# Layer 0 of a two-layer network: half of the scan's sources made by ScalarE and VectorE, small products on GpSimd, PSUM banks assigned by the planner

## The chip, the cores and the metric

The kernel runs on one core of a Trainium2 chip. A core has five engines that work from their own queues, each in order: TensorE (PE, matmuls; its weight loads are listed apart as PEld), VectorE (DVE), ScalarE (ACT), GpSimd (POOL) and SyncE (SP, which issues the DMAs here). They wait for each other through semaphores. On-chip data lies in SBUF, and the matmuls write to PSUM, which has eight banks of 128 x 512 float32. Everything is float32. The metric is the time of one execution on the device in microseconds (us); less is better.

## The reference

The input x is 2 x 2048 x 256 (batch, time, channel). Two layers are applied, each as `x = x + attn(norm(x)) + ffn(norm(x))`. Only layer 0's first branch and its expert network are touched in what they compute with; layer 1 is the larger part of the time.

```python
def _L0_attn_ref(x, W_z, W_params, conv_w, W_dt, b_dt, A_log, D, W_out):
    z = x @ W_z.T
    params = x @ W_params.T                    # dt_unproj (64), unused (16), C (16)
    dt = softplus(dt_unproj @ W_dt.T + b_dt)
    u = silu(causal_conv4(x, conv_w))
    A = -exp(A_log)                            # 256 channels x 16 states
    A_tilde = exp(dt * A)
    B_tilde = where(abs(A) < 1e-05, dt, (A_tilde - 1.0) / (A + 1e-10))
    h[0] = B_tilde[0] * u[0]
    h[t+1] = A_tilde[t] * h[t] + B_tilde[t] * u[t]
    y = sum_n C[t, n] * h[t, :, n]
    return ((y + u * D) * silu(z)) @ W_out.T

def _L0_ffn_ref(x, controller, f1, f2, bias):  # groups of 16 rows, 64 experts
    perm = one_hot_of_best_row(x @ controller)
    inner = relu(select(x, perm) @ f1 + bias)
    return scatter(inner @ f2, perm)
```

Layer 1 has a two-directional selective scan (512 inner channels, 16 states), a feed-forward network behind it, and a network whose dense weights are made from butterfly factors (made in the kernel while layer 0 runs).

## The kernel before

**Layer 0's scan.** Time is cut into chunks of T = 512 steps, four for each of two batches: eight chunks. A scan (L1182) treats 128 rows, 64 channels x 2 states, over 512 steps. The 256 channels are two halves, e = 0 and 1, of two quarters each, h = 0 and 1. For each half and each of eight pairs of states m there is a pair of scans, so 16 pairs, 32 scans, a chunk and 256 in the layer. The kernel walks all eight m of e = 0 first and then those of e = 1. For each pair:

- `load` (L1154 on): SP loads `cb`, two rows of C broadcast to 64 rows each, and `Gm`, the matrix of the sources;
- `decay` (L1150): ACT writes exp(dt A) into a tile of the ring `a` (five tiles of 2 x 512 a row);
- `source` (L1174): PE multiplies `dw` by `Gm` into a PSUM bank of the ring `ab` (two banks). `dw` holds the step of u (u[t+1] - u[t]) in its upper 64 rows and dt u in its lower 64; `Gm` spreads 64 channels over two states and scales each with the inverse of A, or takes dt u where A is tiny;
- `scan` (L1182): DVE runs (source + state) x decay along time;
- `keep` (L1197): POOL saves the last column for the next chunk, and `product` (L1201): POOL multiplies by `cb`;
- `collect` (L1205): PE adds the two states up into a bank `yacc` (one for each half, from a ring of four).

**Around it.** `prepare` makes a chunk's inputs one chunk ahead: projections (PE), `cv`, the convolution (ACT for the first tap, L949, DVE for three more, L962, all in SBUF), silu (L977), softplus (L998), dt u (DVE, L1020), the step of u (DVE, L1029) and a copy of dt u into the lower rows of `dw` (ACT, L1032). `skip` (L1103) starts the bank `yacc` with u D, and the lack products (PE L1115, DVE L1118, PE L1122) correct for the term that the scan leaves out. `gates` and `finish` multiply by silu(z) and by W_out. `prologue` normalizes rows (DVE, L81) and picks the best rows. `experts` runs eight groups of experts: masks (DVE, L680), turned by PE and copied by ACT (L692, L699), gathered rows (L718, L727), two matmuls with a relu (L762, L772, L796, L808), a store to DRAM (`interd<-stage`), a load in another order (`relay<-interd`), and a matmul that is added to the sum (L843, L850). `butterfly_ops` (POOL L281 to L289, DVE L352) makes the weights for layer 1.

**Layer 1's scan** has the same pattern with other names: rows `bT` scaled by ACT (L1847) or POOL (L1849), transposed by PE into `ab` (L1923), scan (DVE L1936), keep and product (POOL L1949, L1955), sum (PE L1967). Its convolution runs in a PSUM bank (ACT L1625, DVE L1632).

**What sets the order.** Nothing loops on the device. Each piece of work is an operation with an engine, an assumed duration, the operations that it needs, the buffers that it takes (`takes`) and a key, its due time in units of one scan (32 a chunk). `Plan.order` places the operations one by one: of those that are ready it takes, for each engine, the one with the lowest key among those that could start within SLACK of the earliest, and then the engine that can start first. An operation that takes buffers isn't started when its key is more than AHEAD0 = 4 beyond the next scan's. The order found is written out engine by engine, and each engine's queue runs in it. Buffers are rings: the n-th taker of a ring of r waits for the users of the (n-r)-th. PSUM is split into rings of fixed banks: `pp` two (all matmuls that are evacuated at once), `ab` two, `yacc` four.

```python
s = op(PE, 1.0, source, ld, ck.o_dw[e], takes="ab", key=key + h - SOURCE0)
before = op(DVE, 1.25, scan, s, (d0, d1)[h], before,
            pv.o_keep[k] if pv and not ck.first else None, key=key + h)
```

## Time and profile before

| | us |
|---|---|
| median of three runs | 2871.68 (2866.61 to 2884.62) |
| the profiled execution | 2875.17 |
| its span, first to last instruction | 2873.5 |
| layer 0's scans (L1182), first and last start | 51.4 and 919.3 |
| layer 1's scans (L1936), first and last start | 930.7 and 2811.5 |

Busy time of the engines in the whole span: PE 2639.9 us (92%), DVE 2378.0 (83%), POOL 2245.8 (78%), ACT 2153.4 (75%). Matmuls overlap and their ends are modelled, so a busy PE is not PE at its peak. A view by stretch gives, for one stretch of the span, each engine's busy us and number of instructions, the TensorE clock that was granted (1.0 is full speed), the share of time in which the DMA engines were busy, and GB/s. A group of instructions is given as line, engine, operation, output<-inputs, shape and count, then busy us and the mean ns of one, then the idle time just before them and what ended it. A waits line says who waited for whom, us in total, how many times and the longest.

### The profile page before, as it was taken

To read this page: it belongs to the slowest core of one execution; us is meant where nothing else is said; L and a number is where in the kernel's file an instruction comes from. 1 tells how busy PE (TensorE), PEld (TensorE's weight loads), DVE (VectorE), ACT (ScalarE), POOL (GpSimd) and SP (SyncE) were. 2 spreads that over 40 slices of the span, in tenths; PEclk is the share of its full clock that TensorE was granted. 3 is DMA by queue.
4 is the path that set the end of the run, shared out by engine and by line. 5 is a ranking of instruction groups with operands and counts; after the bars stand their busy time and mean duration, and the time that the engine had idled before them with its cause. 6 is when DMAs were issued, how large, how long until landed. Compare 5 with 4: busy or idle time off the path is not lost.

```text
span 2873.5 us, 43499 instructions
## 1 busy us (share of the span) xinstructions
PE 2639.9 (92%) x15268; PEld 1877.2 (65%) x15268; DVE 2378.0 (83%) x2508; ACT 2153.4 (75%) x3302; POOL 2245.8 (78%) x2149
## 2 busy tenths in 40 slices
...
GB/s 222 174 205 193 136 189 205 246 203 152 162 181 122 90 82 53 96 68 56 58 99 49 88 85 69 100 74 71 67 60 74 71 56 82 60 64 58 68 63 48
DMA packets 256203, 308.92 MB, mean 108 GB/s; under 512 B 25264, under 2 KB 190256, under 8 KB 254064
## 3 DMA queue, kind: packets, MB, share of 16 engines
...
## 4 chain that ended last, share of the span: by engine, by line
PE 53%; POOL 16%; DVE 14%; issue 7%; DMA 5%; ACT 4%; SPq 1%; POOLq 0%; DVEq 0%; ACTq 0%
PE ab L1923 10%; POOL a L1955 8%; PE yacc L1967 8%; DVE a L1936 6%; PE ab L1174 5%; PE pp L2151 3%; PE pp L2037 3%; PE pp L1607 3%; POOL a L1201 3%; PE pp L2108 3%; PE yacc L1205 2%; PE pp L1578 2%; PE pp L2219 2%; POOL bT L1849 2%; DMA interd<-stage 2%
## 5 line engine op out<-in xcount | busy, mean ns | idle before, releaser
L1955 POOL TENSOR_TENSOR a<-a,cb 128x1024 f32<-128x1024 f32 x512 | 1218.7, 2380 | 29.6 <-DMA cb<-bcd 0.2
L1936 DVE TENSOR_TENSOR_SCAN a<-a,hc,ab 128x512 f32<-128x512 f32 x768 | 941.6, 1264 | 78.2 <-PE ab L1923 60.2
L1905 ACT ACTIVATE a<-dt,A 128x512 f32<-128x512 f32 x1024 | 679.0, 715 | 44.9 <-PE yacc L1967 28.3
L1923 PE MATMUL ab<-ident,bT 128*128 128x128 f32 x4096 | 622.8, 276 | 59.1 <-DVE a L1936 52.6
L1923 PEld LDWEIGHTS ab<-ident,bT 128*128 128x128 f32 x4096 | 484.0, 141 | 240.0 <-DVE a L1936 149.0
L1967 PE MATMUL yacc<-ident,a 128*128 128x128 f32 x4096 | 563.7, 275 | 18.9 <-POOL a L1955 18.6
L1967 PEld LDWEIGHTS yacc<-ident,a 128*128 128x128 f32 x4096 | 471.7, 141 | 58.0 <-POOL a L1955 30.8
L1847 ACT ACTIVATE bT<-dtuT,BT 128x512 f32<-128x512 f32 x640 | 426.1, 713 | 48.2 <-PE ab L1923 45.4
L1936 DVE TENSOR_TENSOR_SCAN a<-a,ab 128x512 f32<-128x512 f32 x256 | 299.1, 1206 | 48.8 <-PE ab L1923 37.2
L1182 DVE TENSOR_TENSOR_SCAN a<-ab,hn,a 128x512 f32<-128x512 f32 x192 | 241.9, 1274 | 97.9 <-PE ab L1174 96.2
L1197 POOL COPY hn<-a 128x2 f32<-128x2 f32 x128 | 47.2, 369 | 344.4 <-DVE a L1182 323.3
L1201 POOL TENSOR_TENSOR a<-a,cb 128x1024 f32<-128x1024 f32 x128 | 306.1, 2391 | 10.4 <-POOL hn L1197 0.3
L1174 PE MATMUL ab<-dw,Gm 128*128 128x512 f32 x512 | 280.9, 646 | 18.1 <-DVE a L1182 9.5
L1150 ACT ACTIVATE a<-dt,As 128x512 f32<-128x512 f32 x256 | 173.6, 716 | 141.1 <-issue 64.9
L1849 POOL TENSOR_SCALAR bT<-dtuT,BT 128x512 f32<-128x512 f32 x384 | 275.0, 721 | 4.8
L1174 PEld LDWEIGHTS ab<-dw,Gm 128*128 128x128 f32 x512 | 86.6, 197 | 143.6 <-issue 64.9
L1949 POOL COPY hc<-a 128x2 f32<-128x2 f32 x512 | 108.5, 212 | 82.6 <-DVE a L1936 80.1
L1205 PE MATMUL yacc<-a,fold 128*64 128x512 f32 x512 | 141.0, 629 | 5.6 <-POOL a L1201 5.6
L2108 PE MATMUL pp<-xnT,wup 128*128 128x256 f32 x512 | 124.6, 388 | 14.8 <-DMA wup<-wupd 12.2
L2037 PE MATMUL pp<-wout,ygT 128*128 128x256 f32 x512 | 130.6, 380 | 2.0 <-DVE zu L1632 1.9
L1607 PE MATMUL pp<-xnT,winx 128*128 128x512 f32 x256 | 125.8, 597 | 2.8 <-DVE zu L1632 2.7
L1578 PE MATMUL pp<-winz,xnT 128*128 128x512 f32 x256 | 125.0, 595 | 2.7 <-DVE zu L1632 2.7
(200 smaller groups left out, 4146.6 us busy)
## 6 DMA issues: line engine op xcount, KB each, us to landing
cb<-bcd SPq DMA_DIRECT2D x256, 256.0 KB, 3.2
cb<-cd SPq DMA_DIRECT2D x256, 128.0 KB, 3.1
Gm<-Gd SPq DMA_DIRECT2D x128, 128.0 KB, 3.2
...
```

The lines of the kernel that those rows point to most:

```text
L1174: nc.tensor.matmul(R["x", h], R["G"][:, h, :], ck.dw[e][:, h, :], start=True, stop=True)
L1182: nc.vector.tensor_tensor_scan(v, R["x", h], v, 0.0 if ck.first else pv.hn[:, k, h : h + 1], ALU.add, ALU.mult,)
L1201: nc.gpsimd.tensor_mul(v, v, R["cb"].unsqueeze(1).broadcast_to([P, 2, T]))
L1607: nc.tensor.matmul(S["ps"], w["winx"][:, k, e * P : (e + 1) * P], ck.xnT[:, k, :], start=(k == 0), stop=(k == 1),)
L1847: nc.scalar.activation(t, ck.dtuT[:, q, :], AF.Copy, scale=v)
L1849: nc.gpsimd.tensor_scalar(t, ck.dtuT[:, q, :], v, 1.0, ALU.mult, ALU.mult)
L1905: nc.scalar.activation(R["a"][:, h], ck.dt[:, e0 + h], AF.Exp, scale=w["A"][:, e0 + h, n : n + 1],)
L1923: nc.tensor.transpose(R["b", h][:, q * P : (q + 1) * P], ck.bT[n, q][:, e * P : (e + 1) * P], c.ident,)
L1936: nc.vector.tensor_tensor_scan(v[:, step], v[:, step], b[:, step], 0.0 if ck.first else pv.hn[:, e, n : n + 1], ALU.mult, ALU.add,)
L1955: nc.gpsimd.tensor_mul(v, v, ck.cb[n].unsqueeze(1).broadcast_to([P, 2, T]))
L1967: nc.tensor.matmul(ck.y[e][:, tb * P : (tb + 1) * P], v[:, tb * P : (tb + 1) * P], c.ident, start=False, stop=(n == NS - 1), is_transpose= ...
L2037: nc.tensor.matmul(S["ps"][:, n * D : (n + 1) * D], ck.ygT[:, e, q * P : (q + 1) * P], ck.w["wout"][:, e, :], start=(e == 0), stop=(e == 3),)
```

## The change

- **Sources.** The scans of a chunk now go through the halves in turn: for each m first e = 0, then e = 1. For e = 0 the source is the matmul as before. For e = 1, ACT copies the step of u (now in all 128 rows of `dw[1]`) into a bank with a scale for each row (`scaled`), and DVE adds `dv` (dt u, in all 128 rows) times a 0/1 factor in the same bank (`rest`). `cb` and `Gm` are loaded once for both halves, and `Gm` exists only for e = 0.
- **Pool.** `ON_POOL = "RRRRRR"` puts six kinds of work from DVE on POOL: the expert masks, dt u of both halves, the step of u of both halves, and the normalization in layer 0's prologue. The second copy of the step (`step_twice`) is there too.
- **Convolution** of layer 0 works in a PSUM bank instead of SBUF; silu of u is an operation for each half, and silu of the gate is one of its own.
- **Banks.** The eight banks are eight fixed tiles. The planner chooses, for each taker, the bank of its list that comes free first, and limits how many whose release isn't placed yet one kind may hold: in layer 0 `pp` up to three of banks 3 to 7, `yacc` banks 0 to 2; in layer 1 `pp` two of banks 4 to 7, `yacc` banks 0 to 3; `ab` two of banks 4 to 7.
- **Rings and due times.** `dt` four tiles instead of three, `dw` four instead of three (a chunk takes three, `dv` among them), `Gm` two instead of three; the lack products' tile comes from the ring `a`. PROD0 1 instead of 0, preparation from key 4 instead of 8, the second batch's experts from key 122, 21 keys each (127, 20), SLACK .08 instead of .15.
- **Layer 1.** `winz` and `wout` lie in another pool and are loaded once layer 0 is done; the two `dt` tiles lie in two pools. All else there is as before, but for the banks and the order.

```diff
-        self.ps = ctx.enter_context(self.tc.tile_pool(name="ps", bufs=2, space=PSUM))
-        self.sums, self.work = sums, work
+    def banks(self, ctx, calls):
+
+        ps = ctx.enter_context(self.tc.tile_pool(name="ps", bufs=1, space=PSUM))
+        self.bank = [ps.tile([P, 512], F32, tag=f"bank{k}", name=f"bank{k}") for k in range(8)]
+        self.calls = calls
...
     def pp(self):
-        return self.ps.tile([P, 512], F32, tag="pp", name="pp", bufs=self.work)
+        return self.bank[self.calls["pp"].pop(0)]
...
-RING0, CB0, LEAD0, LOAD0, SOURCE0, PROD0, COLLECT0, AHEAD0 = 5, 3, 4, 6, 2, 0, 3, 4
-EARLY0, GATE0, PREP0, FIN0, PRO0, EXP0, EXP1, BFLY0 = -2, (10, 15), (8,30), (4, 12), ((-1, 8), (4, 14)), (12, 27), (127, 20), ((8, 110), (114, 200))
+RING0, CB0, XN0, DT0, DW0, GM0, LEAD0, LOAD0, SOURCE0, PROD0, COLLECT0, AHEAD0 = 5, 3, 3, 4, 4, 2, 4, 6, 2, 1, 3, 4
+EARLY0, GATE0, PREP0, FIN0, PRO0, EXP0, EXP1, BFLY0 = -2, (10, 15), (4,30), (4, 12), ((-1, 8), (4, 14)), (12, 27), (122,21), ((8, 110), (114, 200))
...
-SLACK = 0.15
+ON_POOL = "RRRRRR"
+BANKS = {"pp0":((3,4,5,6,7),3),"yacc0":((0,1,2),3),"pp":((4,5,6,7),2),"ab":((4,5,6,7),2),"yacc":((0,1,2,3),4)}
+
+SLACK = .08
...
+        held = {b: None for s, n in self.banks.values() for b in s}
+
+        def free_bank(b):
+            if held[b] is None:
+                return 0.0
+            at = 0.0
+            for u in held[b][0].users[held[b][1]]:
+                if u.end is None:
+                    return None
+                at = max(at, u.end + LATENCY[u.eng])
+            return at
+
+        def choose(o):
+
+            got, at = [], 0.0
+            for t in o.takes:
+                if t not in self.banks:
+                    continue
+                some, most = self.banks[t]
+                have = [b for b in held if held[b] and held[b][1] == t and free_bank(b) is None]
+                if len(have) + [x for x, b in got].count(t) >= most:
+                    return None
+                best = None
+                for b in some:
+                    f = free_bank(b)
+                    if f is not None and b not in [x for y, x in got] and (best is None or f < best[0]):
+                        best = (f, b)
+                if best is None:
+                    return None
+                got.append((t, best[1]))
+                at = max(at, best[0])
+            return at, got
...
-            W["Gd"] = c.dram.tile([P, 4, 8, P], F32, name="Gd")
+            W["Gd"] = c.dram.tile([P, 2, 8, P], F32, name="Gd")
+
+        def rows():
+            W["c1s"], W["smalls"] = inverse(W["As"], "r")
+            nc.vector.tensor_scalar(W["As"], W["As"], -1.0, None, ALU.mult)
...
-        for h in range(4):
+        for h in range(2):
...
-                c.normalize(v, v, *S["m", h], 2)
+                c.normalize(v, v, *S["m", h], 2, nc.gpsimd if ON_POOL[5] == "R" else None)
...
-                nc.vector.tensor_mul(
+                (nc.gpsimd if ON_POOL[0] == "R" else nc.vector).tensor_mul(
...
+        def silu_z():
+            nc.scalar.activation(pv.zs, pv.zs, AF.Silu)
+
+        if i:
+            pv.o_zs = op(ACT, 1.0, silu_z, *pv.o_z, table="silu")
+        us = []
         for e in range(2):
             def conv(e=e):
-                S["c", e] = ap.tile([P, T], F32, tag="cv", name="cv", bufs=rings["cv"])
+                S["c", e] = c.pp()
                 nc.scalar.activation(
...
-            o = op(ACT, 0.67, conv, ck.o_xnT, M["first"], takes="cv")
-            inline("cv", o)
...
-                o = op(DVE, 1.4, tap, o)
+                o = op(DVE, 0.75, tap, o)
...
+
+            def silu_u(e=e):
+                if e == 0:
+                    ck.uw = ap.tile([P, 4, T + 2], F32, tag="uw", name="uw", bufs=rings["uw"])
+                for h in (2 * e, 2 * e + 1):
+                    r = slice(64 * (h % 2), 64 * (h % 2) + 64)
+                    nc.scalar.activation(ck.uw[0:64, h, 2:], S["c", e][r], AF.Silu)
+
+            o = op(ACT, 1.25, silu_u, o, *us, takes="uw" if e == 0 else (), table="silu")
+            c0.users["pp0"].append(o)
+            us.append(o)
...
-                nc.vector.tensor_mul(
+                (nc.gpsimd if ON_POOL[1 + e] == "R" else nc.vector).tensor_mul(
                     ck.uw[64:P, s, 2:], ck.dt[e][0:64, :, 1:], ck.uw[0:64, s, 2:]
...
-                nc.vector.tensor_sub(dw[0:64], ck.uw[0:64, s, 1 : T + 1], ck.uw[0:64, s, 0:T])
+                (nc.gpsimd if ON_POOL[3 + e] == "R" else nc.vector).tensor_sub(dw[0:64], ck.uw[0:64, s, 1 : T + 1], ck.uw[0:64, s, 0:T])
...
-            d = op(DVE, 2.0, delta_u, so, sl)
+            d = op(*((POOL, 2.4) if ON_POOL[1 + e] == "R" else (DVE, 1.5)), delta_u, so, sl)
...
-            d2 = op(DVE, 2.2, step_u, eg, takes="dw")
+            d2 = op(*((POOL, 2.4) if ON_POOL[3 + e] == "R" else (DVE, 2.1)), step_u, eg, takes="dw")
...
-            d3 = op(ACT, 0.99, shift_u, d, d2)
-            ck.o_dw.append(d3)
+            if e == 0:
+                ck.o_dw.append(op(ACT, 0.99, shift_u, d, d2))
+                ck.o_src = list(ck.o_dw)
+            else:
+
+                def step_twice(s=s):
+                    nc.gpsimd.tensor_sub(
+                        ck.dw[1][64:P], ck.uw[0:64, s, 1 : T + 1], ck.uw[0:64, s, 0:T]
+                    )
+
+                def shift_twice(h, s=s):
+                    if h == 0:
+                        ck.dv = ap.tile([P, 2, T], F32, tag="dw", name="dv", bufs=rings["dw"])
+                    nc.scalar.copy(ck.dv[64 * h : 64 * h + 64], ck.uw[64:P, s, 0:T])
+
+                ck.o_step = [d2, op(POOL, 2.4, step_twice, eg, d2)]
+                d3 = op(ACT, 0.99, lambda f=shift_twice: f(0), d, d2, takes="dw")
+                inline("dw", d3)
+                ck.t_dv = d3
+                ck.o_shift = [d3, op(ACT, 0.99, lambda f=shift_twice: f(1), d3)]
+                ck.o_dw += ck.o_step + ck.o_shift
             ck.o_du = d
...
+        ck.t_uw.users["uw"] += [ck.o_uh] + ck.o_dw
...
-                R["t"] = ap.tile([P, 2, T], F32, tag="lk", name="lk", bufs=rings["lk"])
+                R["t"] = sp.tile([P, 2, T], F32, tag="a", name="lk", bufs=rings["a0"])
...
-            s = op(ACT, 1.15, skip, ck.t_uw, M["scans"], takes="yacc", key=key)
+            s = op(ACT, 1.15, skip, ck.o_uw, M["scans"], takes="yacc0", key=key)
             ck.t_y[e] = s
-            inline("yacc", s)
-            m = op(PE, 1.0, lack_mm, ck.o_par, M["cl"], takes=("pp", "pp", "lk"), key=key + 0.2)
+            inline("yacc0", s)
+            m = op(PE, 1.0, lack_mm, ck.o_par, M["cl"], ck.o_du, *ck.o_dw, takes=("pp0", "pp0", "a0"), key=key + 0.2)
+            inline("a0", m)
...
-        for k in range(16):
-            e, m = divmod(k, 8)
-            key = at + 2 * k
+        for j in range(16):
+            m, e = divmod(j, 2)
+            k = 8 * e + m
...
-            def load(e=e, m=m, R=R):
-                R["cb"] = sp.tile([P, T], F32, tag="cb", name="cb", bufs=rings["cb0"])
-                for j in range(2):
...
-            ld = op(SP, 0.2, load, ck.o_cd, *M["G"], takes=("cb0", "G"), key=key - LOAD0)
-            inline("cb0", ld)
+            if e == 0:
+                C = {}
+
+                def load(m=m, C=C):
+                    C["cb"] = sp.tile([P, T], F32, tag="cb", name="cb", bufs=rings["cb0"])
+                    for j in range(2):
+                        nc.sync.dma_start(
...
+                    C["G"] = sp.tile([P, 2, P], F32, tag="G", name="Gm", bufs=rings["G"])
+                    nc.sync.dma_start(C["G"], W["Gd"][:, :, m, :])
+
+                ld = op(SP, 0.2, load, ck.o_cd, *M["G"], takes=("cb0", "G"), key=key - LOAD0)
+                inline("cb0", ld)
...
-                def source(h=h, e=e, R=R):
+                def source(h=h, R=R, C=C):
                     R["x", h] = c.ab()
                     nc.tensor.matmul(
-                        R["x", h], R["G"][:, h, :], ck.dw[e][:, h, :], start=True, stop=True
-                    )
-
-                def scan(h=h, k=k, R=R):
-                    if k == 0 and h == 0:
+                        R["x", h], C["G"][:, h, :], ck.dw[0][:, h, :], start=True, stop=True
+                    )
+
+                def scaled(h=h, m=m, R=R):
+                    R["x", h] = c.ab()
+                    nc.scalar.activation(
+                        R["x", h], ck.dw[1][:, h, :], AF.Copy, scale=W["c1s"][:, 2 + h, m : m + 1]
+                    )
+
+                def rest(h=h, m=m, R=R):
+                    nc.vector.scalar_tensor_tensor(
+                        R["x", h], ck.dv[:, h, :], W["smalls"][:, 2 + h, m : m + 1], R["x", h],
+                        ALU.mult, ALU.add,
+                    )
+
+                def scan(h=h, j=j, k=k, R=R):
+                    if j == 0 and h == 0:
                         ck.hn = ap.tile([P, 16, 2], F32, tag="hn", name="hn", bufs=3)
...
-                s = op(PE, 1.0, source, ld, ck.o_dw[e], takes="ab", key=key + h - SOURCE0)
+                if e == 0:
+                    s = r = op(PE, 1.0, source, ld, *ck.o_src, takes="ab", key=key + h - SOURCE0)
+                    ld.users["G"].append(s)
+                else:
+                    s = op(ACT, 0.62, scaled, *ck.o_step, M["As"], takes="ab", key=key + h - SOURCE0)
+                    r = op(DVE, 0.75, rest, s, *ck.o_shift, key=key + h - 0.6)
+                    ck.t_dv.users["dw"].append(r)
                 inline("ab", s)
                 ck.t_dw[e].users["dw"].append(s)
-                ld.users["G"].append(s)
-                before = op(DVE, 1.25, scan, s, (d0, d1)[h], before,
+                before = op(DVE, 1.25, scan, r, (d0, d1)[h], before,
...
-            def product(R=R):
+            def product(R=R, C=C):
                 v = R["a"]
-                nc.gpsimd.tensor_mul(v, v, R["cb"].unsqueeze(1).broadcast_to([P, 2, T]))
+                nc.gpsimd.tensor_mul(v, v, C["cb"].unsqueeze(1).broadcast_to([P, 2, T]))
...
-            w["winz"] = dp.tile([P, 2, 512], F32, tag="winz", name="winz")
+            w["winz"] = wp.tile([P, 2, 512], F32, tag="winz", name="winz")
...
-        w["z"] = op(SP, 0.2, rows, sw1, *deps)
+        w["z"] = op(SP, 0.2, rows, sw2, *deps)
...
-        w["o"] = op(SP, 0.2, rows, sw1, *deps)
+        w["o"] = op(SP, 0.2, rows, sw2, *deps)
...
-                        ck.dt = ap.tile([P, 4, T], F32, tag="dt", name="dt", bufs=2)
+                        pool = wp if ck.i % 2 else ap
+                        ck.dt = pool.tile([P, 4, T], F32, tag="dt", name="dt", bufs=1)
...
-        "pp": 2, "ab": 2, "yacc": 4, "xp": 1, "lt": 1, "xq": 2, "selT": 1, "pb": 2, "PT": 4,
-        "f1": 1, "f2": 1, "inner": 1, "stage": 2, "relay": 2, "xacc": 4, "xnT0": 3, "zs": 1,
-        "cv": 2, "uw": 1, "par0": 1, "dt0": 3, "dw": 3, "lk": 1, "a0": RING0, "cb0": CB0, "G": 3,
+        "xp": 1, "lt": 1, "xq": 2, "selT": 1, "pb": 2, "PT": 4,
+        "f1": 1, "f2": 1, "inner": 1, "stage": 2, "relay": 2, "xacc": 4, "xnT0": XN0, "zs": 1,
+        "cv": 2, "uw": 1, "par0": 1, "dt0": DT0, "dw": DW0, "lk": 1, "a0": RING0, "cb0": CB0, "G": GM0,
...
+    banks = BANKS
+    pl = Plan(rings, AHEAD0, banks)
+    c.banks(ctx, pl.calls)
```

## The prediction

> **What bounds the kernel now.** I first read the page's busy line and its 40 slices: TensorE is the busiest engine, and the other three lie lower in the first third (layer 0) than in the rest (layer 1). The boundary is dated by the scans: those of layer 0 (L1182) start last at 919.3 us, those of layer 1 (L1936) first at 930.7 us. So the second view is the busy time by stretch: the start (0 to 52), layer 0, layer 1. Columns: stretch, its length, busy us of each engine with the instruction count, granted TensorE clock, DMA share, GB/s.
>
> ```profile
> 0.00:52.00 52.00, 28.10 (x73) 12.38 (x74) 29.86 (x65) 29.03 (x42) 12.22 (x29) 0.70 0.70 227
> 52.00:925.00 873.00, 791.17 (x3282) 371.76 (x3280) 625.80 (x657) 508.95 (x783) 495.31 (x389) 0.96 0.59 182
> 925.00:2873.50 1948.50, 1820.60 (x11914) 1493.10 (x11914) 1722.34 (x1788) 1615.44 (x2479) 1738.23 (x1732) 0.99 0.23 71
> ```
>
> In layer 0 PE is busy 90.6% of the time, DVE 72%, ACT 58%, POOL 57%: one engine is the bound there. In layer 1 it is 93, 88, 83 and 89%: four engines share the load. Adding the four shares gives 2.77 engines busy at once in layer 0 (2421.2 / 873) and 3.54 in layer 1 (6896.6 / 1948.5). Third, the PE groups of 52 to 925, costliest first (busy us, mean ns | idle just before):
>
> ```profile
> L1174 PE MATMUL ab<-dw,Gm 128*128 128x512 f32 x508 | 277.5, 643 | 17.1 <-DVE a L1182 9.5 <-DMA Gm<-Gd 7.4
> L1205 PE MATMUL yacc<-a,fold 128*64 128x512 f32 x512 | 141.0, 629 | 5.6 <-POOL a L1201 5.6
> ```
>
> The largest is the source matmul that this change halves: 254 sources of two records each, 277.5 / 254 = 1.09 us of PE per source. Fourth, the waits, of layer 0 and then of layer 1:
>
> ```profile
> DVE a L1182 <- PE ab L1174: 128.7, 93, 12.4
> ...
> PEld ab L1174 <- DVE a L1182: 52.8, 62, 4.0
> ...
> PE ab L1174 <- DVE a L1182: 9.5, 12, 3.1
> ```
>
> ```profile
> PEld ab L1923 <- DVE a L1936: 149.0, 283, 2.9
> DVE a L1936 <- PE ab L1923: 96.4, 128, 14.6
> ...
> PE ab L1923 <- DVE a L1936: 52.6, 88, 2.7
> ```
>
> Each line gives the waiting row, what it waited for, us in total, times, the longest. The scan waits for a source and the source for a bank that a scan still holds, in both layers: a ring of two banks between PE and DVE.
>
> **The change, part by part (stretch 52 to 925).**
>
> *Sources off PE.* 127 of the 254 sources go: 127 x 1.09 = -139 us of PE, 791 to 652.
>
> *Sources onto ACT and DVE.* Each of the 128 becomes one ACT copy with a scale into a bank and one DVE multiply-add in that bank. The first has no row of its own: SBUF to bank with a scale takes 0.688 us (L1103, 64 rows), SBUF to SBUF 0.72 (L949), bank to bank 0.757 (L1625). I take 0.70: +90 us of ACT. The second has its like in layer 1, one operand in SBUF, the other and the result in a bank:
>
> ```profile
> L962 DVE SCALAR_TENSOR_TENSOR cv<-xnT,cw,cv x48: 719/750/2917, 27.2 to 771.1; 128x512 f32<-128x512 f32 x48
> ```
>
> ```profile
> L1632 DVE SCALAR_TENSOR_TENSOR pp<-xi,pk,pp x128: 726/755/758, 878.1 to 2617.1; 128x512 f32<-128x512 f32 x128
> ```
>
> (min/median/max ns): 0.75 each, +96 us of DVE.
>
> *Convolution into a bank.* The same two rows price it: with all operands in SBUF the tap has the same median but a maximum of 2917 and, in layer 0, a mean of 1299 (54.5 us for 42); in the bank it never passes 758. 42 x 0.75 = 31.5, so -23 us of DVE.
>
> *Masks, norms, dt u and steps to Pool.* DVE loses the groups L680 33.9, L1029 29.0, L81 21.1 and L1020 20.3: -104 us. They too are stretched: L680's median is 684 ns, its mean 1060. POOL gains 32 masks at 1.28 (median of L281, same shape), 32 norms, 16 products and 24 steps (8 of them the second copy). Products and steps run over 1024 elements a partition, as L1201 does (2360 ns): 40 x 2.37 = 95. A 128x256 norm lies between half of L1849 (0.35, 128x512) and L1538 (0.87): I take 0.45, 14 us (11 to 28). POOL +150.
>
> [...]
>
> *Copies and tables on ACT.* 16 copies into dv for 8 copies into dw, at 1.04 (L1032): +8. In the built order ACT loads its function table 148 times instead of 131, because the silu is split in three: 17 x 1.283 (the ACT_TABLE_LOAD rows) = +22.
>
> *DMA.* cb and Gm are loaded once for both halves of the channels: half of 250 x 128 KB and of 124 x 128 KB, 24 of 159 MB. Loads issue ahead of use (3.2 us to landing), and waits on them are few: 13.3 and 6.1 us before the keep copy (L1197), 7.4 before the source (L1174). I count nothing for their being fewer; 27 us is what all present ones cost together.
>
> *Clock.* Stretches of layer 0 show it following PE's load:
>
> ```profile
> 275.00:385.00 110.00, 102.76 (x438) 50.78 (x438) 80.34 (x89) 74.99 (x126) 48.57 (x39) 0.97 0.56 171
> 385.00:495.00 110.00, 93.73 (x388) 45.15 (x389) 78.36 (x86) 58.17 (x88) 60.53 (x50) 0.91 0.64 188
> ```
>
> At 93% busy it is 0.97, at 85% 0.91. With PE busy a little over 80% I take 0.91 against the present 0.96, 5% on 652: +33 us of PE.
>
> [...]
>
> *Sum for layer 0.* PE 652 + 33 = 685; ACT 509 + 90 + 8 + 22 = 629; DVE 626 + 96 - 23 - 104 = 595; POOL 495 + 150 = 645. Together 2554, nothing far ahead any more. How well four such queues overlap decides. At layer 0's present 2.77 it takes 921 us, at layer 1's 3.54 722 (712 without the clock term). I choose 3.25, nearer to layer 1, since the load is now shaped like layer 1's, but below it, because layer 0's expert chain runs through DRAM (PE waits 29.2 us for relay, ACT 17.2 for stage) and takes more table loads per us: 2554 / 3.25 = 786, **-87 us**.
>
> *Change of chunk.* Two channel halves in turn keep both halves' tiles to the chunk's end. A chunk now uses three tiles of the dw ring of four (two of three before), so dv of the next chunk waits for the last scaled copy of this one; the lack products wait for dv, and since their tile now comes out of the decays' ring, the next chunk's first decay waits for them. After the last scaled copy stand two dv copies (2 x 1.04), two skips (2 x 0.69, L1103), four lack matmuls (23.4 us for 32, L1115: 0.73 each, 2.9) and a decay (0.72): 7.1 us, while DVE has one multiply-add and two scans left (3.3). That leaves the scans 3.8 us apart or more at each of seven changes, 27 us; queues in front of these steps can double it, other work can fill it. Nothing of the sort stands in the trace of before. Of 0 to 55 I take **+25**.
>
> *Start.* The first scan (51.4 us) now stands behind three subtractions and a product on POOL (4 x 2.37 = 9.5) where DVE needed 1.22 each for one of either; and the first four lack products stand before it on DVE (they follow it now). Against that, the next scans (57.5 and 64.0) no longer wait for the lacks in between. Between 0 and +10, I take +4.
>
> *Layer 1: banks by schedule.* The same work in the same seam (52 PE and 31 DVE instructions of layer 1 stand ahead of layer 0's last, in both orders). But sources and the other matmuls now draw from four common banks: the built order gives sources three in turn while nothing else needs one. That attacks the waits shown above: at best PE's own 52.6 us go. With PE at 93% and POOL at 89% something else is soon late (POOL's product, L1955). A bank lent to a source can be missed by an evacuation; the list is also re-sorted with a narrower slack. I bound that by 1%, +20. Of -53 to +20 I take **-25**.
>
> Sum: -87 + 25 + 4 - 25 = -83. The profiled run took 2875.2 (span 2873.5 and 1.7 around it), the median of the three is 3.5 lower: 2871.7 - 83 = **2789 us**.
>
> **Rivals.**
>
> *Deep overlap:* layer 0 reaches layer 1's rate (722 or less) and the banks bring 40 or more: -151 + 10 + 4 - 40 = -177, about 2695 (below 2715). For it: layer 1 runs so, with the same two-bank idea. Against: the DRAM chain.
>
> *The ring sets the pace:* PE is relieved, but scans still wait one after another for a source, now through ACT, then DVE; POOL's wait for scans (323.3 us, L1197) shows how much of layer 0 hangs on them. Rate 2.9 for the same work: 881, +8; with the other terms (+25 + 4 - 25): about 2884 (2843 to 2900). That would be a change that relieves PE and doesn't shorten the layer. Against: DVE's 128.7 us wait is on PE's in-order queue, from which half the sources vanish.
>
> *Slower, ACT blocked by banks:* the scaled copy waits on ACT for a bank. Behind it in the same queue stand the decays of later scans, the expert evacuations (L699, L727, L808) and the table loads; DVE waits for the decays, PE for the evacuated banks. Today's waits of sources for a bank are 62.3 us (52.8 + 9.5) for 254, 0.25 each, longest 4.0; at that price 128 cost ACT 31 us. If ACT is otherwise engaged 90% of the time (629 / 0.9 = 699), layer 0 becomes slower by over 1% from (873 + 29 - 4 - 699) / 128 = 1.55 us per copy (the other terms leave +4); at 2 us it is 955: 2872 + 82 + 4, about 2958.
>
> **Chances.** Forecast (2715 to 2843) 0.60; deep overlap 0.14; ring 0.13; ACT blocked 0.13. For 8 in 10 the range takes part of both neighbours: 2690 to 2870. About 1% is what a measurement here can tell from no change (three runs before spread 0.6%); 2843 to 2900 is within it. Faster 0.74, same 0.13, slower 0.13.
>
> **What will show it.** Layer 0's last scan near 860 us instead of 919; PE in layer 0 near 80% with some 140 us fewer source matmuls; scaled copies at 0.70, multiply-adds and taps at 0.75 with no maxima near 3 us; POOL above 80%; clock near 0.91; a gap of some 4 us in the scans at each change of chunk; in layer 1 fewer PE waits on L1936's successor. I am wrong if ACT's waits for DVE in front of the scaled copies pass 1.55 us each, if DVE's wait for sources stays above 130 us, or if layer 1 moves by more than 50.

## The result, and the profile after

The changed kernel takes 2862.1 us (median; 2856.6 to 2873.0) against 2872.7 of the kernel before, measured together on the same chips: ratio **0.9963**, 95% interval 0.9952 to 0.9974. It is faster by 10.5 us, where the forecast was 83. Line numbers below are those of the changed kernel: L1251 is the source matmul, L1257 the scaled copy, L1262 the multiply-add, L1271 the scan, L1187 the lack matmul, L1190 the lack product, L1299 the collecting matmul, L863 the stage copy of an expert's output and L898 the matmul on the relay tile; in layer 1 L2018 is the source, L2031 the scan.

The busy time by stretch of the changed kernel: start, layer 0, layer 1. The columns are those shown before.

```profile
0.00:56.00 56.00, 30.10 (x80) 12.46 (x80) 24.22 (x64) 26.06 (x37) 34.14 (x48) 0.73 0.72 234
56.00:910.00 854.00, 713.30 (x3018) 349.73 (x3019) 595.48 (x695) 604.63 (x929) 584.93 (x476) 0.90 0.49 153
910.00:2860.00 1950.00, 1819.50 (x11912) 1499.00 (x11910) 1727.57 (x1787) 1623.03 (x2489) 1732.76 (x1730) 0.99 0.23 71
```

Layer 0 became 19 us shorter, the start 4 longer, layer 1 did not move. PE lost 78 us of busy time in layer 0, as the step wanted, but the four engines now add up to 2498.3 us in 854, 2.93 at once, where 3.25 was forecast. With 3.25 the same work would have taken 769 us, 85 less; the forecast gave 25 of them to the changes of chunk, apart from this quotient.

The PE groups of layer 0 after (56 to 910): half the source matmuls are gone, and each of the rest, like the collecting matmul, takes longer (665 ns against 643, 673 against 629) at the granted clock of 0.90 (0.96 before).

```profile
L1299 PE MATMUL bank<-a,fold 128*64 128x512 f32 x512 | 154.4, 673 | 30.1 <-POOL a L1295 30.1
L1251 PE MATMUL bank<-dw,Gm 128*128 128x512 f32 x252 | 143.3, 665 | 12.1 <-DVE a L1271 7.6 <-ACT stage L863 1.8 <-ACT PT L754 1.2
```

The waits of layer 0 after (56 to 910):

```profile
POOL hn L1291 <- DVE a L1271: 193.7, 62, 11.1
DVE lk L1190 <- PE bank L1187: 62.3, 14, 13.5
...
ACT stage L863 <- DMA interd<-stage: 44.5, 11, 11.5
...
DVE a L1271 <- PE bank L1251: 42.4, 32, 7.5
...
PE bank L898 <- DMA relay<-interd: 40.4, 12, 6.7
...
DVE bank L1262 <- ACT bank L1257: 24.5, 16, 4.7
...
ACT bank L1257 <- DVE a L1271: 18.2, 18, 4.3
```

The wait that bounded the kernel before, the scan's for a source, fell from 128.7 us to 42.4, and 24.5 of the multiply-adds for their scaled copies. In its place stand a wait of the lack products for their matmuls (9.4 us before, at L1118), and of the stage copy and the relay matmul for their DMAs (17.2 and 29.2 us before).

The scans show where these are. The table adds up, from the trace, the 32 scans of each of layer 0's eight chunks (from the first start to the last end) and the scan-free gaps between chunks, for both kernels:

| us | before | after |
|---|---|---|
| first scan starts | 51.4 | 56.7 |
| inside the eight chunks | 861.7 | 729.6 |
| in the seven gaps between them | 7.3 | 117.3 |
| layer 0's last scan ends | 920.6 | 903.5 |
| from there to layer 1's last scan | 1892.2 | 1896.5 |

The chunks became 132 us shorter and the changes of chunk 110 us longer. The longest gap is the first, 128.0 to 162.5. The timeline of the changed kernel there, PE, then ACT, then DVE (start, duration, engine and line, in brackets the idle time ahead of it and what ended it):

```profile
148.09 1.12 PE L1187 MATMUL bank<-par,cl 16*128 16x512 f32 x2
159.81 2.07 PE L1187 MATMUL bank<-par,cl 16*128 16x512 f32 x2 [10.59 <-ACT stage L863]
...
146.85 1.41 ACT L1175 ACTIVATE bank<-uw,D 64x512 f32<-64x512 f32 x2 [4.65 <-DVE zs L1311]
158.47 1.28 ACT L863 COPY stage<-bank 128x512 f32<-128x512 f32 x2 [10.21 <-DMA interd<-stage]
159.65 2.56 ACT L1224 ACTIVATE a<-dt,As 128x512 f32<-128x512 f32 x4
...
161.91 0.69 DVE L1190 TENSOR_TENSOR lk<-bank,uw 128x512 f32<-128x512 f32 x1 [11.90 <-PE bank L1187]
162.52 2.45 DVE L1271 TENSOR_TENSOR_SCAN a<-bank,hn,a 128x512 f32<-128x512 f32 x2
```

It reads backwards: the scan waits for the lack product and the decay, the product for the second pair of lack matmuls, these for a bank, the bank for a stage copy on ACT, and the copy 10.2 us for the DMA that stores an earlier expert output out of one of the two stage tiles. The decays (L1224) stand behind the same copy on ACT.

### The profile page after: what moved, and what is told of

It reads as the page before. It is cut to its first block, busy times and chain, and to the rows that moved or that the text cites. A ratio compares the mean times of both kernels' runs of the same rounds, so it can differ in the third digit from the quotient of the medians.

```text
span 2860.1 us, 42532 instructions
## 1 busy us (share of the span) xinstructions
PE 2562.9 (90%) x15008; PEld 1861.2 (65%) x15008; DVE 2347.3 (82%) x2545; ACT 2253.7 (79%) x3455; POOL 2351.8 (82%) x2253
## 4 chain that ended last, share of the span: by engine, by line
PE 45%; POOL 22%; DVE 13%; issue 8%; ACT 6%; DMA 5%; SPq 1%; POOLq 0%; DVEq 0%; ACTq 0%
POOL a L2050 11%; PE bank L2018 8%; PE bank L2062 7%; DVE a L2031 4%; PE bank L2246 3%; POOL a L1295 3%; PE bank L2132 3%; PE bank L2203 3%; POOL bT L1944 3%; PE bank L1701 2%; PE bank L1672 2%; PE bank L1299 2%; PE bank L2314 2%; DVE a L1271 2%; DMA interd<-stage 2%
## 5 line engine op out<-in xcount | busy, mean ns | idle before, releaser
L2031 DVE TENSOR_TENSOR_SCAN a<-a,hc,bank 128x512 f32<-128x512 f32 x768 | 930.6, 1260 | 80.0 <-PE bank L2018 62.6
L2018 PE MATMUL bank<-ident,bT 128*128 128x128 f32 x4096 | 613.8, 276 | 33.5 <-DVE a L2031 25.1
L2018 PEld LDWEIGHTS bank<-ident,bT 128*128 128x128 f32 x4096 | 486.7, 142 | 184.1 <-issue 67.3
L2062 PE MATMUL bank<-ident,a 128*128 128x128 f32 x4096 | 565.5, 275 | 33.1 <-POOL a L2050 32.7
L2062 PEld LDWEIGHTS bank<-ident,a 128*128 128x128 f32 x4096 | 470.4, 141 | 77.9 <-POOL a L2050 51.0
L2031 DVE TENSOR_TENSOR_SCAN a<-a,bank 128x512 f32<-128x512 f32 x256 | 295.6, 1202 | 43.4 <-PE bank L2018 34.9
L1295 POOL TENSOR_TENSOR a<-a,cb 128x1024 f32<-128x1024 f32 x128 | 301.8, 2358 | 10.4 <-POOL hn L1291 0.3
L1944 POOL TENSOR_SCALAR bT<-dtuT,BT 128x512 f32<-128x512 f32 x384 | 274.7, 720 | 14.0 <-ACT dtuT L1895 7.5
L1271 DVE TENSOR_TENSOR_SCAN a<-bank,hn,a 128x512 f32<-128x512 f32 x192 | 242.9, 1276 | 38.3 <-PE bank L1251 25.1
L1224 ACT ACTIVATE a<-dt,As 128x512 f32<-128x512 f32 x256 | 174.4, 715 | 21.4 <-PE bank L1299 18.7
L1291 POOL COPY hn<-a 128x2 f32<-128x2 f32 x128 | 27.1, 212 | 194.5 <-DVE a L1271 193.7
L1299 PE MATMUL bank<-a,fold 128*64 128x512 f32 x512 | 154.4, 673 | 30.1 <-POOL a L1295 30.1
L2044 POOL COPY hc<-a 128x2 f32<-128x2 f32 x512 | 107.8, 211 | 82.0 <-DVE a L2031 79.7
L1251 PE MATMUL bank<-dw,Gm 128*128 128x512 f32 x256 | 145.9, 667 | 12.5 <-DVE a L1271 7.6
L2203 PE MATMUL bank<-xnT,wup 128*128 128x256 f32 x512 | 125.5, 387 | 15.2 <-DMA wup<-wupd 12.5
L2132 PE MATMUL bank<-wout,ygT 128*128 128x256 f32 x512 | 128.4, 382 | 3.3 <-ACT h L2323 2.7
L1701 PE MATMUL bank<-xnT,winx 128*128 128x512 f32 x256 | 127.6, 604 | 1.1 <-ACT xnT L1516 0.7
## 6 DMA issues: line engine op xcount, KB each, us to landing
cb<-cd SPq DMA_DIRECT2D x128, 128.0 KB, 3.0
Gm<-Gd SPq DMA_DIRECT2D x64, 128.0 KB, 3.0
```

The lines of the kernel that those rows point to most:

```text
L1271: nc.vector.tensor_tensor_scan(v, R["x", h], v, 0.0 if ck.first else pv.hn[:, k, h : h + 1], ALU.add, ALU.mult,)
L1295: nc.gpsimd.tensor_mul(v, v, C["cb"].unsqueeze(1).broadcast_to([P, 2, T]))
L1299: nc.tensor.matmul(ck.y[e][64 * h : 64 * h + 64], W["fold"], R["a"][:, h], start=False, stop=(m == 7), skip_group_check=True,)
L1944: nc.gpsimd.tensor_scalar(t, ck.dtuT[:, q, :], v, 1.0, ALU.mult, ALU.mult)
L2018: nc.tensor.transpose(R["b", h][:, q * P : (q + 1) * P], ck.bT[n, q][:, e * P : (e + 1) * P], c.ident,)
L2031: nc.vector.tensor_tensor_scan(v[:, step], v[:, step], b[:, step], 0.0 if ck.first else pv.hn[:, e, n : n + 1], ALU.mult, ALU.add,)
```

## The experiments

Four theories of where the forecast's gain went. **A**: the lack products' tile, now out of the decays' ring and tied to the next chunk's copies of dt u, couples the chunks. **B**: POOL's pieces come late. **C**: the stage copy holds a bank while it waits for its DMA; the tile is what is short. **D**: it is the written order. The planner counts a DMA's landing at 2.4 us (`LATENCY`) after an issue of 0.1 to 0.3; the profile of the changed kernel has median landings of 3.0 to 5.3 us for the kinds of layer 0, and the chain that leads into the first gap has one of 8.7 (the stage store issued at 150.4). Each engine's queue runs in order, so an instruction that is placed too early holds up all behind it, as the stage copy above holds up the decays.

All ratios are to the kernel before, with their 95% intervals. "Layer 0" is from the first scan's start to the last one's end, "gaps" as above, "seam" from there to layer 1's first scan, all read from the traces. These three columns are of one profiled execution each, which can lie off the kernel's median (e1 6 us above it, e13 5, e7 10). The kernel before was timed again with each group of runs, at 2870.5 to 2876.3 us, so medians of different groups (e1 to e4, e5 to e8, e9 to e12, e13 to e16, e17 and e18) compare to some 6 us; the ratios allow for that. Line numbers of the edited kernels are off by one, or by some twenty where the sources are on PE; the names tell which row is which.

| | median us | ratio | layer 0 | gaps | seam |
|---|---|---|---|---|---|
| before | 2872.7 | 1 | 869.2 | 7.3 | 10.2 |
| after | 2862.1 | 0.9963 (0.9952–0.9974) | 846.8 | 117.3 | 12.8 |
| e1 control, dt ring 3 | 2866.1 | 0.9977 (0.9963–0.9991) | 852.2 | 151.1 | 14.3 |
| e2 lack tile | 2836.7 | 0.9871 (0.9854–0.9887) | 821.9 | 9.9 | 13.7 |
| e3 four stage tiles | 2833.7 | 0.9867 (0.9849–0.9885) | 811.5 | 107.8 | 13.5 |
| e4 dt u, steps on DVE | 2849.2 | 0.9915 (0.9895–0.9934) | 829.4 | 75.9 | 13.3 |
| e5 lack tile + stage | 2837.6 | 0.9876 (0.9855–0.9897) | 822.8 | 27.7 | 13.7 |
| e6 landing 5.0 | 2838.4 | 0.9878 (0.9855–0.9900) | 804.8 | 122.9 | 12.4 |
| e7 banks of layer 1 fixed | 2890.0 | 1.0064 (1.0031–1.0098) | 857.3 | 113.4 | 13.5 |
| e8 sources on PE | 2875.3 | 1.0010 (0.9997–1.0023) | 855.3 | 108.0 | 12.6 |
| e9 landing 5.0, layer 0 | 2832.5 | 0.9852 (0.9836–0.9869) | 813.7 | 124.1 | 11.3 |
| e10 before, landing 5.0 | 2868.5 | 0.9985 (0.9974–0.9996) | 848.5 | 12.6 | 27.1 |
| e11 = e8 + landing | 2861.8 | 0.9960 (0.9945–0.9974) | 841.7 | 122.7 | 14.3 |
| e12 = lack tile + landing | 2817.5 | 0.9807 (0.9792–0.9822) | 783.4 | 3.9 | 37.8 |
| e13 = e12, banks fixed | 2851.2 | 0.9927 (0.9907–0.9946) | 818.7 | 4.3 | 12.2 |
| e14 = e12, sources on PE | 2814.9 | 0.9808 (0.9792–0.9823) | 800.2 | 8.8 | 12.0 |
| e15 = e12 + stage | 2815.7 | 0.9808 (0.9789–0.9827) | 803.4 | 40.6 | 17.1 |
| e16 = e12, norms on DVE | 2811.7 | 0.9801 (0.9783–0.9819) | 797.9 | 3.1 | 12.5 |
| e17 = e14, the six kinds on DVE | 2814.0 | 0.9784 (0.9767–0.9800) | 800.7 | 8.3 | 11.8 |
| e18 = e12, the six kinds on DVE | 2811.4 | 0.9774 (0.9755–0.9792) | 803.3 | 6.4 | 12.2 |

### The gaps themselves: e1 to e5

e1, a control, since the lack tile needs the room of one dt tile:

```diff
-RING0, CB0, XN0, DT0, DW0, GM0, LEAD0, LOAD0, SOURCE0, PROD0, COLLECT0, AHEAD0 = 5, 3, 3, 4, 4, 2, 4, 6, 2, 1, 3, 4
+RING0, CB0, XN0, DT0, DW0, GM0, LEAD0, LOAD0, SOURCE0, PROD0, COLLECT0, AHEAD0 = 5, 3, 3, 3, 4, 2, 4, 6, 2, 1, 3, 4
```

> The changed kernel with the ring of dt tiles back at three (four in the change); it makes the room that the next two runs need and is their control. All theories: within 15 us of the changed kernel's 2862, scan gaps at the seven changes of chunk still near 117 us in all.

e2, e1 and the lack products in a tile of their own, their matmuls no longer behind the copies of dt u:

```diff
-                R["t"] = sp.tile([P, 2, T], F32, tag="a", name="lk", bufs=rings["a0"])
+                R["t"] = ap.tile([P, 2, T], F32, tag="lk", name="lk", bufs=rings["lk"])
...
-            m = op(PE, 1.0, lack_mm, ck.o_par, M["cl"], ck.o_du, *ck.o_dw, takes=("pp0", "pp0", "a0"), key=key + 0.2)
-            inline("a0", m)
+            m = op(PE, 1.0, lack_mm, ck.o_par, M["cl"], takes=("pp0", "pp0", "lk"), key=key + 0.2)
```

> dt ring three; the lack products have a tile of their own again, their matmuls wait only for the projection (as before the change), and so the next chunk's first decays no longer wait for dv and the steps of u. Theory A (lack tile in the decays' ring couples the chunks): the gaps fall from 117 to under 40 us, time about 2785 (2770 to 2805). Theory B (POOL is late with the steps and dt u): the first scaled copies still wait for them, gaps stay over 90, time over 2845. Theory C (a bank held by the expert store keeps PE's queue): gaps over 80, time over 2835.

e3, e1 and four stage tiles instead of two:

```diff
-        "f1": 1, "f2": 1, "inner": 1, "stage": 2,
+        "f1": 1, "f2": 1, "inner": 1, "stage": 4,
```

> dt ring three; four tiles for the experts' store instead of two, so that ACT's evacuation waits less for the store to land. Theory C: the gaps fall by a third or more (117 to under 80), ACT's wait for the store from 44 to under 15 us, time about 2825. Theories A and B: gaps within 15 us of 117, time within 15 us of the control.

e4, the changed kernel with dt u and the steps on DVE again:

```diff
-ON_POOL = "RRRRRR"
+ON_POOL = "RVVVVR"
```

> dt u and the first copy of the step of u of both halves back on DVE; the second copy of the step stays on POOL. Theory B: gaps fall under 60 us, time about 2805. Theory A: dv still waits for the last scaled copy and the decays for the lack products, gaps within 25 us of 117; time 2850 to 2880, since DVE's stretched products come back (some 50 us of DVE).

The control is 4 us slower than the changed kernel. e2 takes the gaps away, as A has it (151 to 10), but layer 0 gains only 30 us on the control, and the time is 2836.7 where A expected 2785: the chunks grow from 701 to 812 us. In e1's gaps PE is busy for 107 of the 151 us, some 43 of them with the experts' matmuls; in e2 this work lies inside the chunks. e3 gains 41 in layer 0 and leaves the gaps at 108 (151 in the control), so C is right about the time more than about the gaps. A gap in the scans is not lost time as such; other work fills most of it. In e4 the gaps fall to 76 and the kernel gains 13, with 32 us less of POOL and 40 more of DVE: outside what either A or B expected, and not a sign that DVE was short, nor that POOL alone is the cause.

e5, e2 and a third stage tile (cb ring of two for room):

> Both cures of the runs before together: the lack products in a tile of their own (lack matmuls no longer behind the copies of dt u) and a third stage tile for the expert store; dt ring of three as in the control, cb ring of two to make room. Measured alone against the control of 2866.1 us: the first 2836.7 (-29.4), the second 2833.7 (-32.5). If the tile that couples the chunks (theory A) and the bank held by a stage copy that waits for its DMA (theory C) are two losses, the gains add: about 2866 - 62 = 2804, layer-0 end near 842 us. If both only open the same place (the first lack matmuls of a chunk), it is about 2830, end near 868. I expect between, 2812.

The two don't add up: 2837.6 against 2836.7 and 2833.7, where the sum would have been 2804. That fits the theory that they open the same place; it doesn't prove it, since e5 has three stage tiles where e3 has four, and a smaller ring of cb.

### The order: e6, e9, e10, e12

e6 alters one number, the planner's landing; e9 does it for layer 0 alone; e10 does the same to the kernel before; e12 is e9 and e2 together:

```diff
-LATENCY = (0.25, 0.2, 0.12, 0.15, 2.4)
+LATENCY = (0.25, 0.2, 0.12, 0.15, 5.0)
```

```diff
+        o.lat = self.lat if eng == SP else LATENCY[eng]
...
+    pl.lat = 5.0
     r, x1_stores, ops0 = layer0(
...
+    pl.lat = LATENCY[SP]
```

> The changed kernel with one number of its planner altered: the time that the planner adds for a DMA's landing is 5.0 us instead of 2.4, so that instructions which need a DMA are placed later in their engine's queue; the computation is the same. Theory D: the in-order queues stand still because the written order puts DMA-fed instructions where the planner thinks the data are there, while landings of 4 to 9 us were seen (stage copy 44.5 us in 11 waits, relay matmul 40.4 in 12). Then the stage copy's and relay's waits fall by over half and the time by 20 to 40 us against the changed kernel's 2862: 2822 to 2842. If the place in the order does not matter because the tile itself is what is short (theory C), or the loss lies in the lack tile (A), the time stays within 8 us of 2862.

> The changed kernel, planner's DMA landing 5.0 us for the operations of layer 0 alone, 2.4 for those of layer 1. With 5.0 everywhere layer 0's last scan ended at 864.6 us (903.5 in the changed kernel) but layer 1 took 1902.5 (1883.8). Theory D (the written order of layer 0 is what loses the overlap): layer 0 ends near 865, layer 1 takes 1884 again, time 2823 +- 6. If the seam between the layers gives it back (layer 1's time grew because layer 0 ended early, not because of its own order): near 2838.

> The kernel before with the same edit of its planner (5.0 us for layer 0's DMAs). Two theories of why the changed kernel overlaps less than forecast. D1: the changed order alone suffers from the landings that are taken too short (before, PE's work hid them: stage copy 17.2 us of waits against 44.5): before moves by less than 10 us, 2863 to 2873, and the change is then worth about 45 us. D2: both orders suffer alike: before gains 25 to 40 too (2832 to 2848), and the change is worth as little as measured, 10 to 20 us.

> The two causes together: lack products in a tile of their own (alone 2836.7, control 2866.1) and layer 0's DMA landings planned at 5.0 us. If they are separate losses: 2866 - 29 - 39 = 2798. If both only fill the same standstill at the chunk's change, as the lack tile and the stage tiles together did (2837.6 against 2836.7 and 2833.7): 2820 to 2835. I expect 2810.

D holds in the main. In e9 the same instructions with the same tiles, in another order, take 33 us less in layer 0 and 30 in all (2832.5, between its two expectations). The landings had not become longer than before the change (median of `interd<-stage` in layer 0: 4.3 us before, 3.3 after); what grew were the waits for them. The two waits named fell, as expected, by over half, from 44.5 and 40.4 us (waits of e9, up to 900):

```profile
ACT stage L864 <- DMA interd<-stage: 16.4, 6, 6.4
...
PE bank L899 <- DMA relay<-interd: 10.4, 7, 3.2
```

The gaps remain (124 us): again they are not the measure. With the larger number in layer 1 too, that part was 15 us longer (e6 1914.9 us from layer 0's end to the last scan, e9 1899.5; one pair).

e10 is D1's forecast in its total (-5.0 us), but not cleanly: its layer 0 became 20.7 us shorter and the seam 16.9 longer. What is firm: the edit is worth 5 us to the kernel before and 30 to the changed one, and the difference between the two grows from 10.5 to 36.

In layer 0, e12 adds up in full: 783.4 us, 63 less than the changed kernel and 86 less than before, more than the 62 that were forecast for the layer with its changes of chunk (its last scan starts at 834.6, the forecast said 860). The seam then gives 25 us back, and the total, 2817.5, falls between the two expectations: layer 1's first scan waits until 873.7. The traces show where the seam's time goes. From layer 1's first projection (L1795; L1701 before) to its first scan takes 23 to 51 us in all twenty kernels. Where the seam is 10 to 15 us, that projection starts 19 to 38 us before layer 0's last scan ends; in e15 it starts 6 us before, in e12 just as that scan ends, and in e10 0.8 us after.

How much a change of order alone can do is shown by e7 and e13 below: they alter only the banks of layer 1, and layer 0 became 10.5 and 35.3 us longer. So one pair of runs 30 us apart would prove little. But the longer landing shortened layer 0 in all five pairs (e6 and e9 against after, e10 against before, e11 against e8, e12 against e2: 42, 33, 21, 14 and 38 us), and the lack tile in both of its pairs (e2 against e1, e12 against e9: 30 and 30).

### What the moves between engines are worth: e8, e11, e14, e16 to e18

e8 leaves the changed kernel but for the sources: all by matmul, no dv, no second step.

```diff
-                if e == 0:
-                    s = r = op(PE, 1.0, source, ld, *ck.o_src, takes="ab", key=key + h - SOURCE0)
-                    ld.users["G"].append(s)
-                else:
-                    s = op(ACT, 0.62, scaled, *ck.o_step, M["As"], takes="ab", key=key + h - SOURCE0)
-                    r = op(DVE, 0.75, rest, s, *ck.o_shift, key=key + h - 0.6)
-                    ck.t_dv.users["dw"].append(r)
+                s = r = op(PE, 1.0, source, ld, ck.o_dw[e], takes="ab", key=key + h - SOURCE0)
+                ld.users["G"].append(s)
```

> The changed kernel with the sources of both halves of the states as matmuls again (Gm for all four quarters, a dw ring of three, no dv copies and no second step on POOL); halves of channels in turn, masks, norms, dt u and the first steps on POOL, taps in banks stay. It puts some 127 x 1.09 = 139 us of PE back and takes 89 us from ACT, 94 from DVE and 15 from POOL (8 x 1.89). If PE set layer 0's pace before and the move of the sources is what shortened the chunks (the prediction's step): PE needs about 850 us at a clock of 0.96 and at its 90.6% of before layer 0 takes 925 to 940, time 2920 to 2945. If the sources were not the bound and the chunk changes are the loss (no dv, so no lack matmul behind the copies): under 2850.

> All sources as matmuls (as in the run with 2875.3 us), with layer 0's DMA landings planned at 5.0 us. The step that takes half the sources off PE was worth 13 us at 2.4. If the order hid its worth, it is larger here: this kernel stays above 2855 (PE 790 us busy in layer 0 can hardly fit 830 us) while the changed kernel with the same planner comes to 2823, a difference of 30 or more. If PE was never what held the layer, the two differ by 13 again: about 2836.

> Both losses mended, and all sources as matmuls on PE. Its difference to 2817.5 is what the move of the sources is worth when the order does not hide it. By the prediction (PE is the bound of the layer) layer 0 cannot take less than its 790 us of PE at 91%, 865: last scan near 905 to 915, time 2855 to 2870, so the move is worth 40 to 50. If PE was not the bound it is within 15 of 2817.

e8 fits neither of its readings. e11 comes out as its first one has it (above 2855, 29 us behind e9 where 30 or more was expected), e14 as its second (within 15 of 2817). The move of half the sources, the first step of the change and of the prediction, is worth 13 us in the order as built (e8 against after), 29 with the landing corrected (e11 against e9) and nothing, -2.6 us, when both losses are mended (e14 against e12). In e14 layer 0 itself is 17 us longer than in e12; the seam is 26 shorter. And e8 has no dv at all and yet 108 us of gaps: dv is not what couples the chunks.

e16 undoes one move to POOL in e12, e17 and e18 all six of `ON_POOL`, in e14 and in e12:

```diff
-ON_POOL = "RRRRRR"
+ON_POOL = "RRRRRV"     (e16)
+ON_POOL = "VVVVVV"     (e17, e18)
```

> Both losses mended and layer 0's 32 norms back on VectorE: POOL loses 39 us (32 x 1.23), DVE gains 15 to 21. If POOL's late arrivals still hold the layer (theory B; POOL 589 of 810 us busy), 5 to 15 us faster: 2803 to 2812. If no engine is the bound and only the order counts, within 6 of 2817 in either direction.

> Both losses mended, all sources on PE, and masks, norms, dt u and steps back on VectorE: what is left of the change in layer 0 is the order (halves of channels in turn), the taps and the choice of banks. If the moves to POOL shorten the layer (the prediction's -104 us of DVE): DVE rises from 504 to some 610 of 800 us, scans and POOL's products come later, time 2830 to 2860. If the order alone did it: within 8 of 2815, that is 2807 to 2823.

> Both losses mended, half the sources on ScalarE and VectorE as in the change, but masks, norms, dt u and steps on VectorE. DVE has then 603 + 104 = 707 us (more where the pieces are stretched beside POOL) in some 800, 88%. If DVE becomes the layer's bound: layer 0 near 830 instead of 783, time 2840 to 2860, and the moves to POOL are what lets the sources leave PE. If nothing is bound: within 10 of 2817.

e16's gain of 6 us (2 by the ratios) is within what both expectations allow, though its first scan does come 5 us earlier (47.3). e17 and e18 are as their second readings have it: the six kinds of work cost the kernel nothing where they were, on DVE (e17 is 0.9 us under e14, e18 6.1 under e12; 7 and 9 by the ratios). Here too layer 0 and the seam share it out: e18's layer 0 is 20 us longer than e12's, its seam 26 shorter. At the prediction's prices the move costs POOL 46 us more than it saves DVE (150 against 104). The rows bear out that POOL is slower (1.89 to 1.22 us for the step, medians of e14 and e17); the times show no gain from the move and a loss of 9 us at most. The busy time by stretch over layer 0 of e12, e14, e17 and e18, in this order:

```profile
52.00:836.00 784.00, 676.81 (x2984) 329.20 (x2981) 595.84 (x699) 603.59 (x923) 582.96 (x478) 0.92 0.53 167
```

```profile
53.00:853.00 800.00, 758.55 (x3275) 366.96 (x3274) 504.91 (x571) 536.64 (x805) 572.89 (x471) 0.98 0.56 176
```

```profile
52.00:856.00 804.00, 760.84 (x3280) 367.64 (x3280) 601.45 (x658) 538.47 (x803) 478.16 (x390) 0.98 0.56 173
```

```profile
47.00:847.00 800.00, 689.70 (x3015) 336.82 (x3013) 691.62 (x783) 616.91 (x941) 484.68 (x391) 0.93 0.53 164
```

Four quite different loads (PE 677 to 761, DVE 505 to 692, POOL 478 to 583, sums of 2373 to 2483) take 784 to 804 us. With the sources on PE that engine is 95% busy, as in layer 1, at a clock of 0.98. The PE work that takes 791 us in the kernel before takes 759 at this clock and fits into 800 us, against 873 before: PE was the busiest engine there, but not what made the layer 873 us long. Of the four only e12 is shorter, by 16 to 20 us; e13 shows that the order alone can move more.

The view that says so was there for the kernel before: the chain, cut to most of layer 0 (57 to 845), by line. First the kernel before, then e17, then e18.

```profile
by line: PE ab L1174 14.0%; issue 9.6%; POOL a L1201 8.6%; PE yacc L1205 6.6%; DMA interd<-stage 6.2%; PE pp L843 5.6%; PE pp L718 4.7%; DMA relay<-interd 3.8%; DMA Gm<-Gd 2.3%; DMA cb<-cd 2.2%; PE pp L762 2.1%; DVE a L1182 2.1%; PE pp L922
```

```profile
by line: PE bank L1231 22.4%; PE bank L1274 11.2%; PE bank L899 7.3%; PE bank L774 5.8%; DMA relay<-interd 4.6%; PE bank L852 3.8%; PE bank L818 3.7%; issue 3.6%; POOL a L1270 3.0%; PE bank L1305 2.8%; DMA interd<-stage 2.6%; PE bank L1117 
```

```profile
by line: POOL a L1295 8.7%; issue 8.2%; DVE a L1271 7.5%; PE bank L1251 6.5%; PE bank L1299 6.4%; PE bank L899 4.8%; PE bank L774 3.7%; PE bank L818 2.6%; DMA interd<-stage 2.6%; PE bank L852 2.3%; POOL bft L330 2.2%; ACT selT L783 2.2%; DV
```

In the kernel before the source matmuls (L1174) are 32% of layer 0's length in busy time, but 14.0% of its chain; DMAs stand in it with 14.5% in the lines named. In e17 (sources L1231) PE's lines come to 57%: there it is the bound. In e18, with half the sources gone, none is: POOL's product, DVE's scan and PE follow one another, and the layer is no shorter.

### The banks of layer 1: e7, e13

```diff
-"pp":((4,5,6,7),2),"ab":((4,5,6,7),2)
+"pp":((4,5),2),"ab":((6,7),2)
```

> The changed kernel with layer 1's banks dealt as before, two for the sources and two for the other matmuls, instead of four chosen by the schedule; layer 0 as changed. The prediction gave the choice of banks -25 us (then about 2887 here); layer 1 was 1882.0 us long before and 1883.8 after, so I now expect no difference: layer 1 within 6 us of 1884, time 2856 to 2868.

> The kernel with both losses mended (lack tile of its own, layer 0's landings planned at 5.0 us: 2817.5) with layer 1's banks dealt two and two. If the choice of banks is worth something of itself, this is 25 or more slower again: 2843. If the +28 of the run before came from one place of its order (second chunk of layer 1, 135.7 us instead of 108.6, where a norm waits for a DMA), the chunks from the third on take the same as in all others (1646 to 1651 us together) and the time stays within 10 of 2817.

e7 missed, and e13 came out as the first of its theories has it: the fixed banks cost 28 and 34 us. Yet layer 1 itself shows little of it. From its third chunk on it takes 1645.8 us before, 1646.0 after, 1651.4 in e7, 1640.3 in e12 and 1651.3 in e13. The profiled executions are 38 and 39 us apart. Of e7's 38, 10 are in layer 0 and 27 in layer 1's second chunk, 135.7 us against 108.6 (its first is 9 shorter), the rest in the later chunks and behind the last scan; of e13's 39 on e12, 35 are in layer 0 and 11 in the later chunks, while seam and first two chunks give 9 back. In e7's second chunk (1047 to 1183) a norm waits for a DMA and the transposes for the norm:

```profile
PE bank L1509 <- DVE xn L82: 8.8, 3, 7.2
...
DVE xn L82 <- DMA yfd<-xn: 6.8, 1, 6.8
```

The kernel before has fixed banks and 110.2 us at this place; e12, with banks by schedule, has 139.8 (after a first chunk of 101). So this stall goes with the written order, which changes with every edit, and not with fixed banks as such. Layer 1's first two chunks together take 256 and 257 us in e7 and e13 and 230 to 244 in all others, the kernel before among them: a loss that the fixed banks have in the changed order alone. Whether the banks have a worth beside that was not separated: layer 0, whose banks e7 and e13 leave alone, moved as much as layer 1.

### A third stage tile on top: e15

e12 and a third stage tile:

> Both losses mended and a third stage tile (cb ring of two to make room). If the stage tile is a loss of its own (ACT waits 10.7 us for the expert store and PE 14.4 for the relay in the mended kernel), up to -15: 2802 to 2812. If the planned landing has already taken it, within 5 of 2817.

Within 2 us of e12, with layer 0 20 us longer and a seam 21 shorter. So no loss of the stage tile's own is seen where the landing is planned right; the smaller ring of cb may hide one.

## Why the prediction was wrong

*Sources off PE, clock.* Right in kind, and the sources in size: 252 source records instead of 508, -134 us (forecast -139); the granted clock 0.90 (0.91). But PE came to 713 us (685): its other work grew by 56, where the clock term had 33. The trace's clock record has 174.1 us at half speed in this stretch, 78.5 in that of before. e14 and e12 show it again: 127 sources fewer, and PE falls by 82 us only (758.55 to 676.81), the collecting matmul going from 624 to 659 ns while the clock goes from 0.98 to 0.92.

*Prices.* The rows of single instructions in the changed kernel (min/median/max ns):

```profile
L1257 ACT ACTIVATE bank<-dw,rc x128: 668/691/723, 56.2 to 897.2; 128x512 f32<-128x512 f32 x128
```

```profile
L1262 DVE SCALAR_TENSOR_TENSOR bank<-dv,rsmall,bank x128: 721/731/757, 59.0 to 901.5; 128x512 f32<-128x512 f32 x128
```

```profile
L1017 DVE SCALAR_TENSOR_TENSOR bank<-xnT,cw,bank x48: 723/755/756, 30.2 to 771.3; 128x512 f32<-128x512 f32 x48
```

```profile
L82 POOL TENSOR_SCALAR xp<-xp,mv,rs x32: 1215/1230/1735, 11.4 to 452.3; 128x256 f32<-128x256 f32 x32
```

```profile
L1073 POOL TENSOR_TENSOR uw<-dt,uw x16: 1992/1996/2069, 44.4 to 798.7; 64x1024 f32<-64x1024 f32 x16
```

Copy, multiply-add and taps are as forecast (0.70, 0.75, 0.75, and the taps' maximum fell from 2917 to 756). The norm on POOL was mis-sized: 1.23 us against 0.45, outside its bounds of 0.35 and 0.87 (the row that fits best is the costlier one, L1538); 32 of them are 39 us, not 14. Products over 64 rows take 2.0 and steps 1.89, not the 2.37 of 128 rows. Since other POOL pieces also became shorter (the keep copy's mean fell from 369 to 212 ns, that of the butterfly's 128x512 product, L281 before, from 1460 to 1338), POOL has 585 us, not 645. DVE is 595 (595), ACT 605 (629). The engine sums were good to 2% in all: 2498 against 2554.

*The rate of 3.25.* **This is the step that failed**, and with the changes of chunk it carries layer 0's part of the error. The two profiled executions differ by 13 us, 70 short of 83: 40 are missing in layer 0 (-22 us by the scans, against -87 + 25), 29 in layer 1 with its seam (+4 against -25), 1 at the start. The quotient itself is further off: 2498 / 3.25 = 769, 85 us under the 854 measured, changes of chunk included. "How well four such queues overlap decides" was put, and then a number between two layers was chosen from the shape of the load. The runs show that the rate is not set by the load's shape: with the same sums (within 2%) it is 2.93 in the built order and 3.14 in e12, and with three other loads it is whatever makes some 800 us (2.97 in e14, 2.96 in e17, 3.10 in e18). In its place stand the order that the planner writes with landings counted too short (33 us in layer 0, e9) and the lack tile (30 us against its control, e2; 30 more on top of e9, e12); mended together they take layer 0 past its forecast. The DRAM chain was named as the reason to choose below 3.54; its waits were 29.2 and 17.2 us before and 40.4 and 44.5 after, and that they would grow was not asked.

*Half the sources as what the layer is worth.* That "one engine is the bound there" was read from 90.6% busy and from the scan's 128.7 us of waits. e14 and e17 keep all sources on PE and take 800 us. The kernel before with the longer landing takes 848.5 (e10). The 48 us between e10 and e17 lie in what e17 has in common with the changed kernel: the halves of channels in turn with their loads made once, the taps in banks, the shared banks of layer 0, and the due times. These were not taken apart.

*Change of chunk.* The mechanism was half right, and its size off: gaps of 117 us instead of 27 to 55, through the lack tile in the decays' ring, but not through dv (108 us without it in e8), and with the stage copy's DMA in the middle, which the chain forecast did not have. Their cost, though, is not their length: taking them away brings 30. That the lack products are the coupling is shown by e2 (gaps 151 to 10).

*Start.* Right: the first scan at 56.7 instead of 51.4, +5 where +4 (0 to 10) was forecast.

*Layer 1's banks, -25.* Wrong: 1892.2 us from layer 0's last scan to the last of all before, 1896.5 after. Of the waits that it attacked PE's for a bank did fall, the scan's for a source did not. Over 1185 to 2800, inside layer 1 in both, the kernel before:

```profile
PEld ab L1923 <- DVE a L1936: 127.2, 236, 2.9
DVE a L1936 <- PE ab L1923: 71.1, 108, 4.0
...
PE ab L1923 <- DVE a L1936: 45.8, 76, 2.7
...
1185.00:2800.00 1615.00, 1536.66 (x10130) 1261.69 (x10129) 1472.24 (x1506) 1388.09 (x2125) 1483.45 (x1474) 1.00 0.23 70
```

and the changed kernel:

```profile
DVE a L2031 <- PE bank L2018: 74.9, 91, 1.9
...
PEld bank L2018 <- DVE a L2031: 57.8, 110, 2.8
...
PEld bank L2062 <- POOL a L2050: 39.4, 58, 1.6
...
PE bank L2018 <- DVE a L2031: 21.8, 44, 2.6
...
1185.00:2800.00 1615.00, 1536.88 (x10125) 1268.27 (x10124) 1477.43 (x1506) 1377.75 (x2109) 1475.80 (x1468) 1.00 0.23 70
```

PE's 173 us of waits became 80, the scan's 71 stayed at 75, and PE did the same 1537 us of work in the same 1615. POOL's product is late more often (39.4 us of waits at L2062, 25.4 before at L1967), as the forecast's own caution said; the weight of that caution should have been the whole term.

*Rivals.* "The ring sets the pace" comes nearest in its number (rate 2.9; 2862 lies in its 2843 to 2900), but not in its cause: the scan's waits for sources fell to 42.4 us. "ACT blocked by banks" is refuted: 18.2 us of waits for 128 scaled copies, 0.14 us each against the 1.55 at which it would decide. "Deep overlap" did not come, nor did e12 reach it in layer 0 (783 us against its 722). None of the three signs of being wrong came up (0.14 us of waits a copy, 42.4 us for sources, layer 1 moved by 4): they watched single waits, and the loss was in none of these. POOL, at 68% of layer 0, stayed under the 80% that was to show the forecast.

*What stays open.* Why layer 0 takes some 800 us in e18, where no engine is over 87%, was not settled; its chain only shows that no line has 9% of it. Nor is it settled why the order of e10 and e12 has layer 1's first projection so late, or how much of each difference between two of these kernels is the edit and how much the order that came with it.
